# Preparing batch 1 of the first attention during the maxima-only stage

## The chip, the cores and the metric

The kernel runs on one core of one Trainium2 chip. The metric is the device time of one execution in microseconds. All tensors are float32.

## The reference

The program computes four layers on x of shape (2, 1024, 128), each followed by a residual sum and a layer norm: a softmax attention with 16 heads of 8 dimensions, a two-layer local attention with feed-forward parts, a causal attention with rotary positions, and a mixture of experts. The change touches only the first of them:

```python
q = (x @ Wq).reshape(n, s, H, DH)          # n=2, s=1024, H=16, DH=8
k = (x @ Wk).reshape(n, s, H, DH)
v = (x @ Wv).reshape(n, s, H, DH)
attn = einsum('nqhd,nkhd->nqkh', q, k) / sqrt(DH)
attn = softmax(attn, axis=-2)              # over the keys
z = einsum('nqkh,nkhd->nqhd', attn, v).reshape(n, s, d) @ Wout
x = layernorm(x + (x + z))
```

## The kernel before

The first attention is the function `first_attention`. It works in 16 units `m`: a unit is one batch (units 0 to 7 are batch 0, 8 to 15 batch 1), a group of four heads, and one half of the 1024 queries. A softmax needs the maximum of each row before the exponentials. So every unit is gone through twice: `max_score` (L226) multiplies queries by keys into PSUM and DVE reduces each 128x512 tile to a maximum (L232); five steps after the last of a unit's maxima, `exp_score` (L258) makes the scores once more, transposed, with the maximum as one more row of the contraction, and ACT takes the exponential (L263). `values` (L270) multiplies the exponentials by the values; ACT copies that out of PSUM (L276, L281) and POOL adds it up (L282).

A unit has 16 steps; in each step two s_max tiles and, from step 21 on (`LATE`), two s_exp tiles are made. Steps 0 to 19 make maxima alone. They, and the steps at the end where only exponentials are left, are taken in pairs:

```python
pairs = LATE - 1 > t or t > END
...
for consume in scores:
    consume()
t += 2 if pairs else 1
```

After the scores of a step come the value matmuls that are due, and then what the table `also` holds for the steps so far: `at(step, f, *args)` enters a call there. The order in which the calls are written is the order on every engine (the schedule is manual, on SP's queue too). Every matmul result takes the next of eight PSUM buffers, `ring`, in turn, and so waits for the consumer of the result eight places before.

Before its scores a batch needs a preparation. `prepare_x` transposes a half of x into `xT` (four 128x128 transposes, one copy at L174), `project` multiplies it by Wq or Wk (one 128x128 by 128x512 matmul and a copy, L180 to L184) into `all0` and `all1`, and `prepare_values` multiplies by Wv (four matmuls, one copy at L213). From `all0` and `all1`, `spread_q` and `spread_k` send each unit's rows by DMA into the padded operands `qm` and `kTb`; this is done 20 steps ahead of each pair of units. For batch 0 the preparation is made before step 0. For batch 1 its six calls to `prepare_x` and `project` are entered at steps 84 to 94, within unit 5, and those to `prepare_values` at steps 132 and 134, within unit 8. After the maxima of a unit, `max_row` (L236) finishes them, `max_shift` (L243 to L246) transposes them, and a DMA puts them into the row of q.

Each float32 matmul of 512 columns shows as two passes in the trace, so 512 s_max tiles are 1024 matmul records.

Of the kernel before, what the change touches and what calls it, by code (L numbers as in the profile page):

```python
# [7 lines left out]
F32 = mybir.dt.float32  # L8
# [4 lines left out]
P = 128  # L13
B = 2
T = 1024
# [32 lines left out]
def transformer_kernel(ctx: ExitStack, tc: tile.TileContext, a, out):  # L48
    nc = tc.nc
# [35 lines left out]
    def transpose_tiles(ps, src, n):  # L85

        for i in range(n):
            nc.tensor.transpose(ps[:, i * P : (i + 1) * P], src(i), ident)  # L88
# [47 lines left out]
    def first_attention(pool, pool2, poolf, brief, psm, loads, experts, ws, tab, begin):  # L136
        def ring(name):
            return psm.tile([P, 512], F32, tag="ring", bufs=8, name=name)
# [19 lines left out]
        xTs, zs, alls, qs = {}, {}, {}, {}  # L158
# [5 lines left out]
        def prepare_x(b, hf):  # L164
            if hf == 0:
                xTs[b] = pool2.tile([P, T], F32, tag="xT", name=f"xT{b}", bufs=1)
                zs[b] = poolf.tile([P, 8, D], F32, tag="z", name=f"z{b}", bufs=1)
                alls[b] = [
                    brief.tile([P, T], F32, tag=f"all{n}", name=f"all{n}{b}") for n in range(2)
                ]  # L170
            ps = ring("ps_xT")
            transpose_tiles(ps, lambda i: x[b, hf][:, i, :], 4)
            part = xTs[b][:, hf * 512 : (hf + 1) * 512]
            (nc.vector.tensor_copy if hf else nc.scalar.copy)(part, ps)  # L174

        def project(b, hf, n):

            ps = ring("ps_qk")
            part = slice(hf * 512, (hf + 1) * 512)
            nc.tensor.matmul(ps, wa[:, n, :], xTs[b][:, part], start=True, stop=True)  # L180
            if n == 0:
                nc.scalar.activation(alls[b][n][:, part], ps, AF.Copy, scale=8.0 ** -0.5)
            else:
                nc.vector.tensor_copy(alls[b][n][:, part], ps)  # L184

        def spread_k(u):

# [17 lines left out]
        def prepare_values(b, hf):  # L205
            ps = ring("ps_v")
            for i in range(4):
                t = hf * 4 + i
                nc.tensor.matmul(
                    ps[:, i * P : (i + 1) * P], xTs[b][:, t * P : (t + 1) * P], wa[:, 2, :],  # L210
                    start=True, stop=True,
                )
            nc.vector.tensor_copy(  # L213
                vps[b][:, hf * 4 : hf * 4 + 4, :, 0:8].rearrange("p t h d -> p (t h) d"),
                ps.rearrange("p (n d) -> p n d", d=8),
            )
# [123 lines left out]
        def at(step, f, *args):  # L340
            also.setdefault(step, []).append((f, args))

        prepares = [(prepare_x, 0), (prepare_x, 1)]
        prepares += [(project, hf, n) for n, hf in ((1, 0), (1, 1), (0, 0), (0, 1))]
        for u in range(1, UNITS // 2):
            at(32 * u - 20, spread_q, u, 0, nc.sync)
            at(32 * u - 20, spread_k, u)
            at(32 * u - 20, spread_q, u, 1, nc.sync)
            for hf in range(2):
                at(32 * u - 4 + 2 * hf, keep_q, 2 * u + hf)  # L350
        for i, (f, *args) in enumerate(prepares):
            at(16 * 8 - 44 + 2 * i, f, 1, *args)
        for hf in range(2):
            at(16 * 8 + 4 + 2 * hf, prepare_values, 1, hf)
        for m in range(UNITS):
            at(16 * m + 15, max_row, m)
            at(16 * m + 16, max_shift, m)
# [16 lines left out]
        ps = ring("warm")  # L374
        for _ in range(2):
            nc.tensor.matmul(ps, qms[3][:, :P], qms[3], start=True, stop=True)
        for f, *args in prepares[:-1]:
            f(0, *args)
            if f is project and args == [1, 1]:
                spread_k(0)  # L380
        spread_q(0, 0, nc.scalar)
        project(0, 1, 0)
        spread_q(0, 1, nc.sync)
        for m in range(2):
            keep_q(m)
        for hf in range(2):
            prepare_values(0, hf)
# [1225 lines left out]
    with tc.tile_pool(name="af", bufs=1) as pf:  # L1613


        brief = tc.tile_pool(name="a0", bufs=1, side="right")
        first = tc.tile_pool(name="l0", reuse_waits="tile", bufs=1, side="right")
        pb = brief.__enter__()

        def at_first():  # L1620
            brief.__exit__(None, None, None)
            return first.__enter__()

        with (
            tc.tile_pool(name="a1", bufs=1) as p1, tc.tile_pool(name="a2", bufs=2) as p2,
            tc.tile_pool(name="psm", bufs=1, space=bass.MemoryType.PSUM) as psm,
            tc.manual_schedule(engines=engines | {mybir.EngineType.SP}),
        ):
            finish = first_attention(
                p1, p2, pf, pb, psm, loads, loads_too, ws, tab, lambda bank: begin(bank, at_first)  # L1630
            )
        with (
            tc.tile_pool(name="l1", reuse_waits="tile", bufs=1) as p1,
            tc.tile_pool(name="l2", reuse_waits="tile", bufs=1) as p2,
            tc.tile_pool(name="psl", reuse_waits="tile", bufs=1, space=bass.MemoryType.PSUM) as psl,
            tc.manual_schedule(engines=engines),
        ):
            left = steps(p1, p2, psl, finish)
        first.__exit__(None, None, None)
# [111 lines left out]
```

## Time and profile before

| | |
|---|---|
| median of three runs | 1090.54 us (1090.28 to 1091.72) |
| profiled execution | 1090.38 us, of it the span of the profile 1088.6 us |
| PE busy | 994.9 us, 91% |
| DVE busy | 802.0 us, 74% |
| ACT busy | 743.9 us, 68% |
| POOL busy | 569.3 us, 52% |
| first s_max to last of the first attention's maxima | about 13 to 403 us |
| one copy of 128x512 out of PSUM | 0.59 us on ACT, 0.69 us on DVE |

The busy times are of the whole program, whose stages differ; a matmul's end is modelled, so that a busy PE is not one at its peak. The times of the timelines are counted from the start of the span.

### The profile page before, as it was taken

The numbers are of one execution on the slowest core, as the hardware profiler recorded it, in microseconds if no ns is written. First come the engines' busy times: TensorE is split into PE (matmuls) and PEld (weight loads), VectorE is DVE, ScalarE is ACT, GpSimd is POOL, SyncE is SP. The second block draws the span as 40 slices with busy tenths as digits, with TensorE's granted clock in tenths as the row PEclk, the third lists the DMA queues.
The fourth block names the chain that finished last, engine by engine and source line by source line (L and its number), as shares of the span: only waits on it lengthen the run. The fifth ranks groups of instructions, "written<-read, shape, count | busy, mean of one in ns | idle before, by whom it ended". The sixth has DMA issues, their size and how long they took to land. (4 is left out here: it accounts for less than half of the span.)

```text
span 1088.6 us, 21891 instructions
## 1 busy us (share of the span) xinstructions
PE 994.9 (91%) x8091; PEld 589.4 (54%) x8091; DVE 802.0 (74%) x1681; ACT 743.9 (68%) x1503; POOL 569.3 (52%) x625
## 2 busy tenths in 40 slices
PE   8999999999999999779889999999787799999991
PEld 4533333333333332356666657676564466689891
DVE  6988878888898886868969678696754387757443
ACT  1488878888888887568878788797763555444442
POOL 4134333434543433678978686786732135408753
PEclk9799999999999999989999999999898899999996
DMA  3111523122220200200101001010000000146883
GB/s 91 33 38 50 147 60 87 42 59 59 60 55 13 79 2 1 74 21 21 31 21 26 21 17 31 21 31 21 16 2 1 0 1 23 42 158 206 307 302 125
DMA packets 57210, 65.09 MB, mean 60 GB/s; under 512 B 9076, under 2 KB 43424, under 8 KB 57104
## 3 DMA queue, kind: packets, MB, share of 16 engines
q1 hardware_dynamic: 53472, 57.40, 17.9%
q0 software_dynamic: 2272, 4.92, 1.3%
q8 instruction: 64, 1.05, 0.4%
q10 hardware_dynamic: 1360, 1.38, 0.4%
q14 instruction: 42, 0.34, 0.1%
HBM read 37.98 MB, written 19.67 MB: 53 GB/s over the span
## 5 line engine op out<-in xcount | busy, mean ns | idle before, releaser
L232 DVE TENSOR_REDUCE mx<-s_max 128x1 f32<-128x512 f32 x512 | 318.2, 684 | 57.1 <-PE s_max L226 52.3
L263 ACT ACTIVATE pr<-s_exp 128x512 f32<-128x512 f32 x512 | 265.6, 602 | 71.1 <-PE s_max L226 58.7
L226 PE MATMUL s_max<-kTb,qm 32*128 32x512 f32 x1024 | 262.9, 642 | 0.5 <-DMA qm<-all 0.5
L282 POOL TENSOR_TENSOR av<-av,avp 128x512 f32<-128x512 f32 x101 | 128.0, 1267 | 245.7 <-ACT avp L281 226.6
L258 PE MATMUL s_exp<-q,kTb 32*128 32x512 f32 x1024 | 253.1, 616 | 0.0
L258 PEld LDWEIGHTS s_exp<-q,kTb 32*128 32x128 f32 x1024 | 101.2, 184 | 88.1 <-DVE mx L232 66.8
L270 PE MATMUL av<-pr,vp 128*32 128x512 f32 x1024 | 137.2, 605 | 0.7 <-ACT pr L263 0.7
L226 PEld LDWEIGHTS s_max<-kTb,qm 32*128 32x128 f32 x1024 | 113.6, 190 | 36.1 <-ACT pr L263 13.5
L755 ACT ACTIVATE pm<-pm,nb,rn 128x128 f32<-128x128 f32 x256 | 105.5, 490 | 0.1
L657 POOL TENSOR_TENSOR t<-raw,tab 128x512 f32<-128x512 f32 x64 | 87.1, 1381 | 19.4 <-DVE raw L625 10.8
L690 POOL TENSOR_TENSOR rn<-rn,neghalf 128x16 f32<-128x16 f32 x32 | 94.0, 2937 | 2.7
L649 DVE TENSOR_TENSOR t<-raw,tab 128x1024 f32<-128x1024 f32 x32 | 40.8, 1273 | 54.7 <-ACT raw L642 54.5
L270 PEld LDWEIGHTS av<-pr,vp 128*32 128x32 f32 x1024 | 20.5, 108 | 98.4 <-ACT pr L263 94.5
L636 PE MATMUL ps_qk<-wqkv,hT 128*128 128x512 f32 x120 | 58.8, 613 | 3.0 <-DVE o L788 2.5
L281 ACT COPY avp<-av 128x512 f32<-128x512 f32 x101 | 60.0, 594 | 1.8 <-PE av L270 0.6
L499 PE MATMUL ps_w<-hnT,w 128*128 128x512 f32 (+1 forms) x96 | 48.3, 635 | 13.1 <-DVE mt L517 9.8
L642 ACT COPY raw<-ps_qk 128x512 f32<-128x512 f32 x60 | 32.2, 589 | 38.1 <-PE ps_qk L636 37.4
L689 POOL TENSOR_SCALAR rn<-rn 128x16 f32<-128x16 f32 x32 | 31.1, 970 | 46.1 <-DVE rn L688 45.6
L1467 ACT ACTIVATE gj<-ps_fc 128x512 f32<-128x512 f32 x39 | 23.3, 597 | 41.2 <-PE ps_fc L1462 39.9
L1482 POOL DMA_INDIRECT yr<-yj,to x39 | 37.4, 958 | 23.1 <-DVE yj L1478 19.3
L688 DVE TENSOR_REDUCE rn<-sq 128x16 f32<-128x1024 f32 x32 | 38.6, 1208 | 9.5 <-ACT sq L664 9.4
L731 PEld LDWEIGHTS ps_sim<-kT,qT 64*64 64x64 f32 x1024 | 28.3, 135 | 31.9 <-issue 15.1
(230 smaller groups left out, 2012.1 us busy)
## 6 DMA issues: line engine op xcount, KB each, us to landing
wj<-ew SPq DMA_DIRECT2D x39, 512.0 KB
xs<-zero SPq DMA_DIRECT2D x8, 1152.0 KB
vh<-vb SPq DMA_DIRECT2D x60, 130.0 KB
xj<-xs SPq DMA_DIRECT2D x39, 72.0 KB
tab<-in_tab SPq DMA_DIRECT2D x2, 1024.0 KB
ew<-in_proj_w SPq DMA_DIRECT2D x8, 256.0 KB
ew<-in_fc_w SPq DMA_DIRECT2D x1, 2048.0 KB
wqkv<-in_wqkv SPq DMA_DIRECT2D x2, 768.0 KB
```

Source lines behind the costliest of these rows:

```text
L226: nc.tensor.matmul(s, q[32 * head : 32 * head + 32, qt * P : (qt + 1) * P], k[32 * head : 32 * head + 32, kh * 512 : (kh + 1) * 512], star ...
L232: return lambda: nc.vector.reduce_max(mx[:, head, qt, kh : kh + 1], s, axis=AX.X)
L258: nc.tensor.matmul(s, k[32 * head : 32 * head + 32, kt * P : (kt + 1) * P], q[32 * head : 32 * head + 32, :], start=True, stop=True,)
L263: return lambda: nc.scalar.activation(pr[:, head, :], s, AF.Exp)
L270: nc.tensor.matmul(ps[32 * h : 32 * h + 32, :], vps[m // 8][:, kt, 4 * g + h, :], pr[:, h, :], start=True, stop=True,)
L281: nc.scalar.copy(part, ps)
L282: nc.gpsimd.tensor_add(avs[m], avs[m], part)
L499: nc.tensor.matmul(ps[:m, n * 512 : (n + 1) * 512], w["w1"][:, n * HID + c0 : n * HID + c0 + m], f["hnT"], start=True, stop=True,)
L636: nc.tensor.matmul(ps[:, k * 512 : (k + 1) * 512], s["hT"], w["wqkv"][:, k * 512 : (k + 1) * 512], start=True, stop=True,)
L657: nc.gpsimd.tensor_mul(s["t2"][:, :, :, lo : lo + 32], raw4[:, :, :, hi : hi + 32], tabls[layer][:, t, 1, :, lo : lo + 32].unsqueeze(2).to ...
L690: nc.gpsimd.tensor_tensor(rn, rn, neghalf.to_broadcast([P, 16]), ALU.pow)
L755: nc.scalar.activation(s["pm"][:, k, :], s["pm"][:, k, :], AF.Exp, scale=s["rn"][:, head : head + 1], bias=s["nb"][:, k : k + 1],)
```

## The change

Batch 1's preparation is entered at steps 1, 3, 5, 7, 9, 11 (transposes and projections) and 13, 17 (values), where only maxima are made. The buffers of the projected q and k are doubled, so that those of both batches stand side by side. All copies of batch 1's preparation are on ACT; before, DVE made five of the eight.

```diff
                 alls[b] = [
-                    brief.tile([P, T], F32, tag=f"all{n}", name=f"all{n}{b}") for n in range(2)
+                    brief.tile([P, T], F32, tag=f"all{n}", name=f"all{n}{b}", bufs=2) for n in range(2)
                 ]
...
-            (nc.vector.tensor_copy if hf else nc.scalar.copy)(part, ps)
+            (nc.vector.tensor_copy if hf and b == 0 else nc.scalar.copy)(part, ps)
...
             if n == 0:
                 nc.scalar.activation(alls[b][n][:, part], ps, AF.Copy, scale=8.0 ** -0.5)
             else:
-                nc.vector.tensor_copy(alls[b][n][:, part], ps)
+                (nc.scalar.copy if b else nc.vector.tensor_copy)(alls[b][n][:, part], ps)
...
-            nc.vector.tensor_copy(
+            (nc.scalar.copy if b else nc.vector.tensor_copy)(
                 vps[b][:, hf * 4 : hf * 4 + 4, :, 0:8].rearrange("p t h d -> p (t h) d"),
                 ps.rearrange("p (n d) -> p n d", d=8),
             )
...
         for i, (f, *args) in enumerate(prepares):
-            at(16 * 8 - 44 + 2 * i, f, 1, *args)
+            at(1 + 2 * i, f, 1, *args)
         for hf in range(2):
-            at(16 * 8 + 4 + 2 * hf, prepare_values, 1, hf)
+            at(13 + 4 * hf, prepare_values, 1, hf)
```

## The prediction

> **What bounds the kernel now.** I read the page's slices first, then the DVE timeline for the time of each unit of the first attention, then timelines and windows of the two places between which the change moves work.
>
> ```profile
> PE   8999999999999999779889999999787799999991
> DVE  6988878888898886868969678696754387757443
> ACT  1488878888888887568878788797763555444442
> PEclk9799999999999999989999999999898899999996
> ```
>
> A slice is 27.2 us. TensorE is near full over the first attention (slices 1 to 16). In the second slice, 27 to 54 us, DVE is full, ACT half idle, and the granted clock falls to 0.7: the stage that makes only maxima is another regime than the rest. The timeline of DVE shows when each unit's 32 maxima are finished (line 236, one per 16 steps):
>
> ```profile
> 35.00 0.19 DVE L236 TENSOR_REDUCE nm<-mx 128x16 f32<-128x32 f32 x1
> 57.14 0.19 DVE L236 TENSOR_REDUCE nm<-mx 128x16 f32<-128x32 f32 x1
> 81.55 0.19 DVE L236 TENSOR_REDUCE nm<-mx 128x16 f32<-128x32 f32 x1
> 105.95 0.19 DVE L236 TENSOR_REDUCE nm<-mx 128x16 f32<-128x32 f32 x1
> 130.36 0.19 DVE L236 TENSOR_REDUCE nm<-mx 128x16 f32<-128x32 f32 x1
> ...
> 160.15 0.19 DVE L236 TENSOR_REDUCE nm<-mx 128x16 f32<-128x32 f32 x1
> ...
> 208.96 0.19 DVE L236 TENSOR_REDUCE nm<-mx 128x16 f32<-128x32 f32 x1
> ...
> 235.58 0.19 DVE L236 TENSOR_REDUCE nm<-mx 128x16 f32<-128x32 f32 x1
> ```
>
> A plain unit takes 24.40 or 24.41 us (81.55 to 105.95 to 130.36). The unit that holds the transposes and projections of batch 1 (steps 84 to 94) takes 160.15 - 130.36 = 29.79; the one that holds its values (steps 132, 134) takes 235.58 - 208.96 = 26.62. In a plain unit no engine is full: eight matmul passes at a time, four exponentials, four maxima and one copy make a round of 2.92 us in which each engine waits for the other, so whatever is put into TensorE's queue lengthens the round.
>
> In the first stage it is otherwise. The DVE timeline again, then windows of all engines (length, then busy us of PE, PEld, DVE, ACT, POOL with instruction counts, granted clock, DMA share, GB/s):
>
> ```profile
> 16.94 18.03 DVE L232 TENSOR_REDUCE mx<-s_max 128x1 f32<-128x512 f32 x30 [0.95 <-PE s_max L226]
> 35.00 0.19 DVE L236 TENSOR_REDUCE nm<-mx 128x16 f32<-128x32 f32 x1
> 35.10 11.02 DVE L232 TENSOR_REDUCE mx<-s_max 128x1 f32<-128x512 f32 x18
> ```
> ```profile
> 15.57:18.98 3.41, 3.41 (x19) 2.56 (x19) 2.46 (x5) 0.00 (x0) 0.73 (x2) 0.53 0.14 24
> 18.98:22.40 3.42, 3.42 (x18) 1.65 (x13) 3.42 (x7) 0.00 (x0) 0.29 (x1) 1.00 0.22 34
> ...
> 25.81:29.22 3.41, 3.41 (x13) 2.72 (x13) 3.41 (x7) 0.00 (x0) 0.00 (x0) 0.50 0.05 10
> ...
> 36.05:39.47 3.42, 3.42 (x17) 2.46 (x16) 3.34 (x7) 0.00 (x0) 0.00 (x0) 0.54 0.51 163
> ```
>
> From 16.94 to 46.12 DVE reduces 48 times without a gap, one each 0.60 us; ACT does nothing until 35.7. PE's busy time is full only because matmul ends are modelled: its clock is at half from 25.81 to 39.47 and DVE still does not wait. So there is PE time to be had here, if PE never falls behind DVE.
>
> **What comes off.** All sixteen matmul groups of batch 1's preparation leave the rounds, with their copies: two groups of four transposes, four projections, two groups of value matmuls. The units give the price with all waits in it: 29.79 - 24.41 = 5.38 us, and 26.62 - 24.40 = 2.22 us, together 7.60. The rounds agree: from one av copy of ACT to the next, 134.30 to 137.22 is 2.92 without, 137.22 to 140.74 is 3.52 with a transpose group, 152.78 to 156.76 is 3.98 with a projection; 2 x 0.6 + 4 x 1.05 = 5.4. The saving lies on the path, since everything after waits for the rounds.
>
> **What goes in.** PE's new order is: four s_max, then one group of the preparation, then four s_max, and so on for seven rounds of two steps; the eighth group (second half of the values) stands behind the 16x128 transpose of unit 0's maxima. Each group takes one of the 8 PSUM buffers of the ring. DVE gets nothing; ACT gets all eight copies, 8 x 0.59 = 4.7 us in a stretch where it is idle for 21 us, so they are hidden. They are not ahead of anything that waits except the last two: the row copy of unit 0 stands behind one values copy (long done) and ahead of the other; the first exponential (40.23) comes 4 us later.
>
> *The start.* The four transposes stand behind the fourth s_max, so the fifth can no longer run beside the fourth. Before, the fourth's last pass starts at 16.34 and the fifth's ends at 17.43, 0.7 us before DVE wants it at 18.14. With the clock at half here (0.53 in the window), a pass holds its rows 0.85 us (16.34 to the next at 17.19), the transposes take about 4 x 0.25 (0.66 for four at full clock, with the last one's tail), then the fifth needs two passes and its tail: 17.2 + 1.0 + 0.85 + 0.6 = 19.65. DVE waits 1.5 us. With full clock the same sum gives 0.6. I take 1.5, by the clock of that window. Nothing gives this back, since DVE is full until 46.12.
>
> *The rounds after it.* DVE needs 4 x 0.60 = 2.39 us. PE at full clock needs about 1.0 for four s_max (sixteen passes of a later round start within 1.9 us) and 1.1 for a projection (1.12 us for its two passes) or a value group (1.16): 2.1 in all, so hidden, 0. At half clock the s_max take 1.7, the group 1.7 + 0.2: 3.6, that is 1.2 us late in each. The cover is thus the clock. I take full: it was full from 18.98 to 25.81 with less work than PE will now have. The first stretch of s_max alone comes only after the first value group, too late to matter.
>
> *The last group.* PE waits for unit 0's maxima anyway (it sat 0.54 us before the transpose); four finished s_max then feed DVE for 2.4 us. Before, the next s_max started at 35.55 and DVE waited 0.08. With the group between, at full clock (1.0) data come at 37.7 against 37.5; at half clock (1.9) about 1.1 late. I take 0.3, between these and near the first.
>
> Other waits: batch 1's x has landed by 8 us (DMA share 1.01 to there, then 0.04), before the transposes at 17; the second pair of buffers for projected q and k removes a reuse and adds no wait; SP's queue and POOL's keep their instructions in order. The buffer of xT is free after the value matmuls of batch 0 at 12.6.
>
> Sum: 1.5 + 0.3 in, plus 0.2 for a second transpose group with little lead, makes 2.0; 7.6 - 2.0 = 5.6 us gained. The profiled execution took 1090.38 us (span 1088.6 and 1.8 around it), the median is 1090.54, so either will do: 1090.4 - 5.6 = **1084.8 us**.
>
> **A rule that speaks against it.** The clock changes in this trace lie on a grid of 3.41 us, and the half rate of 15.57 to 18.98 was ended after a window with 19 s_max passes. In the changed kernel this window has some nine passes and four transposes. If they are too few, the half rate lasts to 22.40: the s_max after the first transposes are ready at 20.2 (2.1 us of waiting instead of 1.5), the second transposes cost 0.6, the first projection about 0.8; with the 0.3 of the last group 3.8 in all, **1086.6 us**. The Trainium skill, "TensorE: Matmul & The Clock Gate", Part 4, says that transposes do not count as activity to the gate, which would be this case; no row of this trace shows it. Part 1 of that page has the gate close after an idle window; here it closed at 25.81 with no idle time on PE, so the trace does not agree that a gap is needed.
>
> **Other rivals.** *The half rate holds through the whole stage.* For it: it held from 25.81 to 39.47 although PE always had an s_max in flight. Against it: there PE waited for buffers, while now it would run without a pause, as it did in 15.57 to 18.98, after which the full rate came. Price: 2.1 + 0.6 + 4 x 1.2 for the projections + 1.2 and 1.1 for the values = 9.8 against 7.6: **1092.6 us**, slower by 2.2. It turns slower only once all of the groups are paid at half rate: without two of them it is a gain.
>
> *The saving is caught by what follows.* If the stage after it waited on a transfer, the end would not move: 1090. Against: DMA moves 1 to 2 GB/s in slices 14 and 15, so nothing is under way when the local layers start, and the chain that ended last has 1% DMA in it. *The two long units are long for another reason*, and stay so: 1092; but among units 2 to 8 they alone are long, and by just what their rounds hold more.
>
> *The later clock.* After 440 us the granted clock in the trace falls to half ten times, for 3.4 or 6.8 us each but for the last. Moving everything by 5.6 us, not a multiple of 3.41, shuffles which work falls in such a window; a window at half costs up to 1.7 us of PE time. Two of these against us give **1088.2**; they may as well go for us.
>
> **How the numbers follow.** Forecast 0.57; half rate one window longer 0.22; later clock 0.08; half rate throughout 0.07; saving caught 0.04; long units stay 0.02. The range goes from the cheap start and one kind window later (7.6 - 0.6 + 1.2 = 8.2 gained) to two groups more at half rate and a bad window on top of the longer half rate (1086.6 + 1.2 + 1.7): 1082.2 to 1089.5. About 0.2%, 2.2 us, is what can be told from no change: faster takes the first three but for a small part, 0.85; within it lie the caught saving, half of the half-rate case and the rests, 0.10; slower 0.05.
>
> **What would show it.** Units 5 and 8 fall to 24.4 each, counted from maximum to maximum. The first unit's maxima finish at about 36.7 instead of 35.00, with DVE waiting once near 18 us for s_max; the clock is full from 19 to past 30 us; ACT has eight copies between 17 and 38. Wrong would be: DVE waits of about a microsecond in each round up to 35 with the clock at 0.5, the first maxima at 40 or later, or a distance from the first maxima to the end of the attention that has not shrunk by 7.6.

## The result, and the profile after

The changed kernel takes 1082.95 us (median of five runs, 1080.18 to 1083.65) against 1090.54 (1088.14 to 1091.72): a ratio of 0.993, 95% interval 0.9918 to 0.9942. Its profiled execution has a span of 1081.2 us, 7.4 less than before.

The page's slices after, 27.0 us each (busy tenths, then the granted clock):

```profile
PE   9999999999999999779989999999787799999891
DVE  5988888887998887778968777695754387757443
ACT  1488888888888887568878788797662565444442
PEclk8999999999999999889999999999898899999996
```

The second slice has the clock back at 0.9 or more: the half rate of the profile before, which its record of the clock puts at 25.57 to 39.22 us, is gone. The first slice has a lower clock than before (8 for 9), since the half rate of the start lasts longer. DVE is full in the second slice as before. The DVE timeline after, a unit's finished maxima in each line (start us, duration, engine, line):

```profile
37.41 0.19 DVE L236 TENSOR_REDUCE nm<-mx 128x16 f32<-128x32 f32 x1
59.39 0.19 DVE L236 TENSOR_REDUCE nm<-mx 128x16 f32<-128x32 f32 x1
...
132.61 0.19 DVE L236 TENSOR_REDUCE nm<-mx 128x16 f32<-128x32 f32 x1
157.01 0.19 DVE L236 TENSOR_REDUCE nm<-mx 128x16 f32<-128x32 f32 x1
...
205.82 0.19 DVE L236 TENSOR_REDUCE nm<-mx 128x16 f32<-128x32 f32 x1
230.23 0.19 DVE L236 TENSOR_REDUCE nm<-mx 128x16 f32<-128x32 f32 x1
```

Unit 5 now takes 157.01 - 132.61 = 24.40 us and unit 8 230.23 - 205.82 = 24.41: the 7.60 us are off. The price is in the first line: 37.41 instead of 35.00. It is paid at the start. These are the first maxima in the same timeline (in brackets the idle time of DVE ahead of the line and its releaser), and the windows between the changes of the clock:

```profile
16.16 1.38 DVE L232 TENSOR_REDUCE mx<-s_max 128x1 f32<-128x512 f32 x2 [0.19 <-PE s_max L226]
19.89 2.48 DVE L232 TENSOR_REDUCE mx<-s_max 128x1 f32<-128x512 f32 x4 [2.36 <-PE s_max L226]
22.93 14.44 DVE L232 TENSOR_REDUCE mx<-s_max 128x1 f32<-128x512 f32 x24 [0.56 <-PE s_max L226]
```
```profile
15.92:19.33 3.41, 3.41 (x15) 1.23 (x12) 1.42 (x3) 0.58 (x1) 0.66 (x2) 0.50 0.14 25
19.33:22.75 3.42, 3.42 (x16) 1.23 (x12) 2.48 (x4) 0.58 (x1) 0.00 (x0) 0.50 0.25 38
22.75:26.16 3.41, 3.41 (x20) 1.05 (x19) 3.23 (x6) 0.62 (x2) 0.00 (x0) 1.00 0.18 30
```

DVE waits once behind each of the two transpose groups, in two windows at half clock; from 22.93 on it does not wait again until 37.41, with four projections and a value group in TensorE's queue, at full clock.

The whole difference of the two profiles, from when maxima finish: the start +2.41, unit 1 (22.14 to 21.98) -0.16, units 5 and 8 -7.60, unit 9 (25.13 to 24.99) -0.14, unit 12 (25.66 to 24.97) -0.69, the other units 0.0; that is -6.18 at the last maxima (411.30 to 405.12; the table of the profile before has these at about 403 us, which is wrong). From there to the end it is 676.06 instead of 677.30, another -1.24.

### The profile page after: what moved, and what is told of

It reads as the page before. It is cut to its first block, busy times and chain, and to the rows that moved or that the text cites. A ratio compares the mean times of both kernels' runs of the same rounds, so it can differ in the third digit from the quotient of the medians.

```text
span 1081.2 us, 21885 instructions
## 1 busy us (share of the span) xinstructions
PE 986.3 (91%) x8091; PEld 579.3 (54%) x8091; DVE 797.5 (74%) x1676; ACT 746.6 (69%) x1508; POOL 569.9 (53%) x625
## 5 line engine op out<-in xcount | busy, mean ns | idle before, releaser
L226 PE MATMUL s_max<-kTb,qm 32*128 32x512 f32 x1024 | 255.6, 624 | 0.5 <-DMA qm<-all 0.5
L226 PEld LDWEIGHTS s_max<-kTb,qm 32*128 32x128 f32 x1024 | 104.4, 185 | 34.2 <-ACT pr L263 15.5
L650 DVE TENSOR_TENSOR t<-raw,tab 128x1024 f32<-128x1024 f32 x32 | 40.1, 1253 | 54.5 <-ACT raw L643 54.4
L1483 POOL DMA_INDIRECT yr<-yj,to x39 | 37.4, 958 | 23.8 <-DVE yj L1479 20.0
```

Of the source, the lines that this page charges most:

```text
L226: nc.tensor.matmul(s, q[32 * head : 32 * head + 32, qt * P : (qt + 1) * P], k[32 * head : 32 * head + 32, kh * 512 : (kh + 1) * 512], star ...
L1483: apart("out", nc.gpsimd.indirect_dma_start(out=yr, out_offset=bass.IndirectOffsetOnAxis(ap=s["to"], axis=0), in_=y, in_offset=None,))
```

## The experiments

The runs e1 to e4, e6, e8 and e9 ran on one chip, r1, r2, e5 and e7 on another. On the first of these the kernel before takes about 1100 us, nearly all of the excess behind the first attention (e1 takes 686.2 us after its last maxima there, the same kernel 675.1 on the other). So times are compared on one chip, or as ratios to the kernel before on that chip; the times of the first attention agree between chips to 0.01 us in a plain unit. The theory throughout is that the start is paid because the transposes stand at a place where DVE has no tile in store, and that it costs more at half clock; the rivals are named with each run.

**The transposes elsewhere.** Run e1 makes them ahead of step 0:

```diff
         for i, (f, *args) in enumerate(prepares):
-            at(1 + 2 * i, f, 1, *args)
+            if f is not prepare_x:
+                at(1 + 2 * i, f, 1, *args)
...
         for hf in range(2):
             prepare_values(0, hf)
+        for hf in range(2):
+            prepare_x(1, hf)
```

> Both transpose groups of batch 1 are moved ahead of step 0, behind the value matmuls of batch 0; all else is as in the changed kernel. Theory (the 2.4 us that the first maxima lose are the transposes standing in the half-rate window and keeping the clock at half for one more window of 3.41 us): the s_max are dense again, the clock is full from about 19.3 us, the first unit's maxima finish at 35.0 to 35.6 instead of 37.41, and the time falls by about 2 us against the changed kernel, to 1081. Rival (each group costs its TensorE time wherever it stands before the first maxima): 1.2 to 2 us of it only move ahead of the first s_max, maxima at 37, the time stays at 1083.

Measured: ratio 0.9916 (0.9894 to 0.9938), first maxima at 34.47, every later unit as in the changed kernel. DVE's first maximum starts 0.8 us later (14.74), its third at 16.41 against 16.16, and from there on it does not wait. The theory holds for the place. For the clock this run shows nothing: in this execution it was never at half between the first s_max and 450 us.

Run e2 leaves them in the stage, four steps later with all the rest:

```diff
-            at(1 + 2 * i, f, 1, *args)
+            at(5 + 2 * i, f, 1, *args)
         for hf in range(2):
-            at(13 + 4 * hf, prepare_values, 1, hf)
+            at(17 + 2 * hf, prepare_values, 1, hf)
```

> The whole preparation four steps later: transposes at steps 5 and 7, projections at 9 to 15, values at 17 and 19, when the ring is full and TensorE is several tiles ahead of DVE. Theory: full clock from about 19.3 us as in the kernel before, no wait of DVE at 18 us, maxima of unit 0 at 35.0 to 35.3; the two value groups stand between the maxima's transpose and the first exponentials and may cost up to 1 us; 1081 to 1082. Rival (groups between s_max tiles stall DVE by 2.4 us wherever they stand): maxima at 37.4, 1083.

Measured: 0.9928 (0.9908 to 0.9949), first maxima at 34.52, no wait of DVE behind a transpose group, and unit 1 at 21.98, so both value groups behind the maxima's transpose cost nothing. DVE from the third maximum on:

```profile
16.39 18.09 DVE L232 TENSOR_REDUCE mx<-s_max 128x1 f32<-128x512 f32 x30 [0.16 <-PE s_max L226]
```

The rival falls: a group between s_max tiles costs nothing once TensorE is ahead. Here the clock was at half from 16.2 to 19.6 and DVE still did not wait.

**Is it the transposes that keep the clock low?** Run e3 turns x by plain matmuls:

```diff
-            transpose_tiles(ps, lambda i: x[b, hf][:, i, :], 4)
+            if b:
+                for i in range(4):
+                    nc.tensor.matmul(
+                        ps[:, i * P : (i + 1) * P], x[b, hf][:, i, :], ident, start=True, stop=True
+                    )
+            else:
+                transpose_tiles(ps, lambda i: x[b, hf][:, i, :], 4)
```

> Batch 1's transposes made as plain matmuls with the identity, in the same places. If the gate does not count transposes as activity, and that kept the half rate to 22.75 us, the clock is now full one window earlier, from about 19.3, though these matmuls have twice the passes: first maxima at 36.8 to 37.5, and the second group and the s_max after it run at full rate. If transposes count as other work does and the window was simply too empty or too interrupted, the clock is full from 22.75 as before, and the longer matmuls at half rate put the first maxima at 38.5 to 39.5.

Measured: 1093.93 us in one execution. Up to the first maxima, at 37.13, the clock is at half from 16.9 to 20.3 alone, one window, and DVE waits 2.65 us behind the first group. (A second window follows from 37.4 to 40.8; unit 1 takes 23.58.) That is what the first theory expected, but run r1 below shows one window with transposes as well, so it proves nothing. Runs e8 and e9 ask the question by itself, with a long row ahead of step 0:

```diff
         for hf in range(2):
             prepare_values(0, hf)
+        long = ring("long")
+        for _ in range(32):
+            transpose_tiles(long, lambda i: x[0, 0][:, i, :], 4)
```

> A look at the clock alone: 128 more transposes of 128x128 in one row ahead of step 0, whose results nobody reads, in the changed kernel. If the gate does not count transposes as activity, the clock, at full before, falls to half within one or two windows of 3.41 us inside the stretch, and the stretch takes about 25 us instead of 17 (0.13 us each at full clock). If it counts them, the clock stays at full through the stretch.

> The same with 64 plain matmuls of 128x128 with the identity (two passes each) in place of the 128 transposes: the same number of passes, about 14 to 17 us at full clock. Both theories have the clock at full through the whole stretch; if it falls here too, the fall in the run with transposes says nothing of transposes.

TensorE's timeline of e8, and two windows within the stretch:

```profile
12.31 14.14 PE L88 MATMUL long<-cst,x 128*128 128x128 f32 x128
```
```profile
19.00:22.00 3.00, 3.00 (x30) 3.00 (x29) 0.00 (x0) 0.00 (x0) 0.16 (x1) 1.00 0.24 37
22.00:25.00 3.00, 3.00 (x30) 3.00 (x29) 0.00 (x0) 0.00 (x0) 0.00 (x0) 1.00 0.22 34
```

The granted clock, the third number from the right, stays at 1.00 over 14.14 us of nothing but transposes (four windows of 3.41 us), as it does over the 14.46 us of matmuls in e9. So transposes of float32 keep a clock up that is already full. Whether they alone bring it back from half, no run shows. The sentence of the Trainium skill that the prediction weighed ("TensorE: Matmul & The Clock Gate", Part 4) does not hold for these transposes.

**The copies.** Run e4 has the new steps with the old engines:

```diff
-            (nc.vector.tensor_copy if hf and b == 0 else nc.scalar.copy)(part, ps)
+            (nc.vector.tensor_copy if hf else nc.scalar.copy)(part, ps)
...
-                (nc.scalar.copy if b else nc.vector.tensor_copy)(alls[b][n][:, part], ps)
+                nc.vector.tensor_copy(alls[b][n][:, part], ps)
...
-            (nc.scalar.copy if b else nc.vector.tensor_copy)(
+            nc.vector.tensor_copy(
```

> The preparation at the new steps, but five of its eight copies on DVE again, as in the kernel before. Theory (the stage is bound by DVE, one maximum each 0.60 us, and ACT is idle): five copies of 0.69 us stand in DVE's queue, 3.0 to 3.5 us later maxima than the changed kernel's, less what of them falls into DVE's waits at 18 and 22 us (one copy at most): maxima at 39.8 to 40.9, 1085.5 to 1086.5. Rival (the copies are hidden by waits that are there anyway): maxima at 37.5, 1083.

Measured: 0.9981 (0.997 to 0.9992); on the same chip 1097.6 us against 1090.46 of e1. First maxima at 37.84, unit 1 at 23.00. Its DVE timeline:

```profile
18.58 2.48 DVE L232 TENSOR_REDUCE mx<-s_max 128x1 f32<-128x512 f32 x4 [0.63 <-PE s_max L226]
20.98 0.68 DVE L174 COPY xT<-ps_xT 128x512 f32<-128x512 f32 x1
21.58 2.48 DVE L232 TENSOR_REDUCE mx<-s_max 128x1 f32<-128x512 f32 x4
```

Each copy takes one turn of 0.60 us in DVE's queue and none falls into a wait: four ahead of the first maxima, 2.4 together, and one behind. In unit 1 the clock was at half from 39.1 to 42.5, and DVE waited another 0.34 at 41.35, so that its 23.00 are not the copy alone. Up to 39.1 the clock was full, and the wait behind the first transposes was the smallest, 0.63. The expectation had the first maxima two to three microseconds later, because it counted from the two-window start; with the copies taken off they would stand at 37.84 - 2.4 = 35.44. It missed the time the other way: 1085.5 to 1086.5 of about 1090.5 is a ratio of 0.9954 to 0.9963, and 0.9981 was measured. Against the profile of e1 e4's is 4.82 us late at the last maxima (407.02 to 402.20) and loses another 1.7 behind them, which nothing here explains.

**The changed kernel once more, beside e1.** r1 is the changed kernel, r2 is e1, on another chip, five rounds.

> The changed kernel itself, to stand beside the next three on one chip. First maxima at 37.4 us if the clock's windows fall as in its first profile (two windows at half from about 16 us), 35.3 to 36 if they fall so that the clock stays full over the transposes, as it did in the run with copies on DVE, where the wait at the first transposes was 0.71 us. Time 0.993 of the kernel before.

> The transposes of batch 1 ahead of step 0, once more and beside the changed kernel. Theory (the transposes between the first s_max cost 2.4 us when they fall into a half-rate window): first maxima at 34.5 as before, 2 to 3 us less than the changed kernel, a ratio of about 0.9975 to it. Rival (the clock's windows fall by chance and mostly well): under 1 us less.

r1: 0.9938 (0.9924 to 0.9951), median 1083.10. r2: 0.9923 (0.991 to 0.9937), median 1081.01: 2.09 us less, with intervals that overlap. DVE in r1, then in r2:

```profile
19.00 16.84 DVE L232 TENSOR_REDUCE mx<-s_max 128x1 f32<-128x512 f32 x28 [1.45 <-PE s_max L226]
35.87 0.19 DVE L236 TENSOR_REDUCE nm<-mx 128x16 f32<-128x32 f32 x1
```
```profile
14.23 19.60 DVE L232 TENSOR_REDUCE mx<-s_max 128x1 f32<-128x512 f32 x32 [1.23 <-PE s_max L226]
33.86 0.18 DVE L236 TENSOR_REDUCE nm<-mx 128x16 f32<-128x32 f32 x1
```

In r1 the half rate lasted one window (17.1 to 20.5), the first transposes still ran at full rate, DVE waited 1.45 us and the second group cost nothing. r2's 32 maxima stand without a gap. The profiles differ by 35.87 - 33.86 = 2.01 at the first maxima and by 1.98 at the last. Not all of this is the edit: batch 0's values are copied from 11.49 us on in r2 and from 11.85 in r1, so 0.36 of it is there before the first s_max. The other 1.65 is what the start costs in r1. The version of e1 and r2 has the lowest time of those tried, by about 2 us against the changed kernel; as the intervals overlap, five rounds make this likely and not certain.

**The parts.** e5 is the kernel before with `bufs=2` for the projected q and k, e7 has besides all of batch 1's copies on ACT, at the old steps. e6 is the changed kernel with one line undone:

```diff
-            at(13 + 4 * hf, prepare_values, 1, hf)
+            at(16 * 8 + 4 + 2 * hf, prepare_values, 1, hf)
```

> The kernel before with only the buffers of projected q and k doubled: steps and engines of the preparation as before. Units 5 and 8 should stay at 29.8 and 26.6 us and the time at that of the kernel before, within 0.2%. If units 9 and 12, which lost 0.14 and 0.69 us in the changed kernel although nothing in them was moved, are shorter here too, the buffers' places are behind that; if they are 25.13 and 25.66 as before, it is something else, such as where the ring's turn or the copies' engine stands.

> The preparation at its old steps (84 to 94, 132 and 134), but with all its copies on ACT and the buffers doubled. Theory (in the rounds the group itself lengthens the round, not the engine of its copy): unit 5 at 29 to 31 us, unit 8 at 26 to 27.5, the time within 1.5 us of the kernel before. Rival (the five copies on DVE were what lengthened the rounds, so that moving them to ACT is the gain): units 5 and 8 near 25, the time 5 us lower.

> One part of the change alone: transposes and projections of batch 1 at the new steps, the two value groups back at steps 132 and 134 (copies on ACT). Theory (each part's price is its own): unit 8 at 26.6 us instead of 24.41, all other units as in the changed kernel, so 2.2 us more than that, a ratio of about 0.9955 to the kernel before; unit 1, at whose border the last value group stood, stays at 22.0, since that group cost nothing. Rival (the last value group delays the first exponentials): unit 1 or the first maxima shorter by 0.3 to 1 us, and the loss only 1.2 to 1.9.

e5: 0.9993 (0.9983 to 1.0003), units 5 and 8 at 29.78 and 26.62, unit 9 at 25.00, unit 12 at 25.67. e7: 0.9993 (0.9982 to 1.0004); unit 5 is the distance of these two lines of its DVE timeline, 29.65, and unit 8 is 26.58:

```profile
130.38 0.19 DVE L236 TENSOR_REDUCE nm<-mx 128x16 f32<-128x32 f32 x1
160.03 0.19 DVE L236 TENSOR_REDUCE nm<-mx 128x16 f32<-128x32 f32 x1
```

So neither the buffers nor the engine of the copies is the gain in the rounds; the group in TensorE's queue is what lengthens a round. The engine matters only where DVE is the bound, as e4 shows. e6: 0.9966 (0.9955 to 0.9977), unit 8 at 26.59, first maxima at 36.41; the values' part is worth its 2.2 us in unit 8. Unit 12 is back at 25.66 in e6, another 0.69, of which below. The rival can't be read from unit 1 of e6 (22.43), where the clock was at half from 38.1 to 44.9. It falls by r1 and e2: with one value group behind the first maxima, and with both, DVE takes the next 18 maxima there without a gap, and unit 1 is 21.98.

## Why the prediction was right

It said 1084.8 us, range 1082.2 to 1089.5, and 1082.95 was measured. It lies in the range, but 1.85 us off the forecast. By its steps:

- *What comes off*, 7.60: exactly that, 5.39 and 2.21. e6 and e7 show the parts and that steps, not engines, do it. (The "sixteen matmul groups" of the text are eight; its sums count eight.)
- *The start*, 1.5 (and 0.2 for the second group): the mechanism was right, DVE waits behind transposes that stand where it has no tile in store. The size depends on where the clock's windows fall, which differs from execution to execution. DVE's idle time behind the first transposes was 0.63 us with full clock (e4), 1.45 with one window at half (r1, e6) and 2.36 with two, where the second group adds 0.56 (the profile after). The text had 0.6 with full clock, 1.5 at half, and 2.1 and 0.6 for the longer half rate. The profiled execution is thus the case of the rival, half rate one window longer; the other two are not. The 0.8 that this rival put on the first projection did not come. The fifth s_max, which the sum had ready at 19.65, reached DVE at 19.89; but DVE was free for it at 17.54, and not at 18.14. (The clock's changes in the profile before lie 0.24 us ahead of the window edges in the text, and the window of half rate to which it gives 19 passes has 17.)

  From the third maximum to the end of unit 0's maxima it is 18.06 us before and 37.41 - 16.16 = 21.25 after: this start cost 3.2 us, against 1.7 in the sum. In r1 and e6 it cost 1.55 (19.61). That the two profiles differ by 2.41 and not by 3.2 is luck: the third maximum came 0.78 us sooner after (16.16) than before (16.94). The change does not do that, since e5, which has the old steps, has it sooner still, and its 30 maxima as dense as before:

```profile
15.92 18.02 DVE L232 TENSOR_REDUCE mx<-s_max 128x1 f32<-128x512 f32 x30 [0.17 <-PE s_max L226]
```

- *The rounds after it*, 0: right; the cover was the full clock, which came back and stayed to past 37 us in the four profiles with these steps (the changed kernel, r1, e4 and e6). The rival of half rate throughout did not appear. The old steps have that half rate each time: 25.6 to 39.2 us before, 23.0 to 40.1 in e5, 26.4 to 40.1 in e7.
- *The last group*, 0.3: measured 0. DVE takes the 18 maxima behind it without a gap. Unit 1 is 0.16 shorter than before, because these take 10.86 us instead of 11.02 (11.01 and 11.02 in e7 and e5, where the clock is at half as well).
- *Nothing else moves*: this missed 0.83 us. Unit 9's 0.14 goes with the doubled buffers (e5, e7 have it; why was not tried). Unit 12's 0.69 goes with the steps of the values. Unit 12 takes 25.66 or 25.67 us in the four profiles with these at 132 and 134 (before, e5, e6, e7), and 24.97 or 24.98 in the others; e6 and the changed kernel differ in that line alone. So the values' new steps gave 2.21 + 0.69 = 2.90, near the 3.1 us by which the ratios of e6 and r1 differ. What is longer in unit 12 is a place where DVE and POOL meet. In the profile before, first POOL, then DVE, then the second of DVE's two steps by itself:

```profile
320.35 1.27 POOL L282 TENSOR_TENSOR av<-av,avp 128x512 f32<-128x512 f32 x1 [1.65 <-ACT avp L281]
```
```profile
320.10 1.60 DVE L118 TENSOR_SCALAR x<-y,ln_mv,ln_rs 128x128 f32<-128x128 f32 x2
```
```profile
320.35 1.34 DVE L118 TENSOR_SCALAR x<-y,ln_mv,ln_rs 128x128 f32<-128x128 f32 x1
```

and DVE at the same place after, and in e6:

```profile
314.62 0.59 DVE L118 TENSOR_SCALAR x<-y,ln_mv,ln_rs 128x128 f32<-128x128 f32 x2
```
```profile
316.24 1.59 DVE L118 TENSOR_SCALAR x<-y,ln_mv,ln_rs 128x128 f32<-128x128 f32 x2
```

The second normalizing step began in the same moment as POOL's addition, and ended only 0.08 us behind it: 1.60 us for the two instead of 0.59. After, both were over at 315.21, 0.12 us into POOL's addition (315.09). e5, e6 and e7, whose unit 12 is long, show the same long step; the runs with a short unit 12 do not have it there, though all thirteen have one such step in unit 11. The Trainium skill names a cause that fits, in "GPSIMD Engine Reference", Specifications: POOL shares its SBUF interfaces with DVE, with contention for DVE instructions of certain kinds. The trace agrees as far as it goes, with 1.34 us for an instruction of 0.34; that this one is of those kinds no run shows. No run moves POOL's addition alone, and how the values' steps shift the meeting of the two four units later was not followed.
- *The later clock*: it was given as two windows either way. From the last maxima to the end it is 1.24 us less, with two half-rate windows near 944 and 1019 us missing after. These are hardly the whole cause: e7 lacks them too and takes 677.1 there. e5 and e7, which have the same steps and ran on one chip, differ by 1.8 (678.9 to 677.1), so 1.24 is no more than what two executions differ by.

With the measured terms the sum is 1090.38 - 7.60 + 2.41 - 0.16 - 0.83 - 1.24 = 1082.96. It meets the changed kernel's profiled execution because the terms are read from the same two profiles, so it shows only that none is left out. The 1.85 us between forecast and result are the rest of larger errors of both signs. The start cost 3.2 instead of 1.7, and the last group -0.16 instead of 0.3, 1.0 too much together; the early third maximum, units 9 and 12 and the rest gave 0.78 + 0.83 + 1.24 = 2.85 that no term had. Of these, units 9 and 12 belong to the change; the 0.78 and the 1.24 are luck. What was forecast of the mechanism, the saving of 7.60 and the wait behind the transposes, was right; the size of the start fits r1 (1.55, though the first transposes ran at full rate there) and is about half of what it was in the profile after.

## What to carry to other kernels

Work on a saturated engine's queue costs its full price in a stage where all engines wait for each other in turn, and nothing in a stage that another engine bounds: read the price from units with and without it, and the cover from that stage alone. Put it where the consumer already has some tiles in store, not behind the first ones, and give its copies to the engine that idles. A price that hangs on the clock is a range, not a number: the same order of work started with no window at half rate (e4), with one (r1) or with two (the profile after). Before reading a start of +2.41 as the price, look where two executions of the same steps differ by themselves: the first maxima of e5 and e7 are 1.07 us apart (33.97 and 35.04).

## What the runs showed of the hardware

Long rows of float32 transposes hold the full clock (14.14 us, e8). The half rate can begin in a stage where TensorE shows no idle time (before, from 25.57 us). It goes in windows of 3.41 us, and it went closely with the number of matmul passes that the trace has in the window before. In the thirteen profiles, up to about 45 us, each fall to half came behind a window with 9 to 15 passes, and none behind one with 16 or more. A half-rate window with 15 or fewer was followed by another each time (11 times); one with 16 or more by the full clock, but for one with 16 in e5 (13 of 14 times). Not every window at full clock with 15 or fewer was followed by half rate, and some records can be missing or fall on an edge, so what is counted stays open. A DVE step that starts together with POOL's addition lasts as long as that: 1.34 us instead of 0.34.
